# A graph-attention layer on one core: norm, softmax and attention of the next group moved to other stages, roots computed on VectorE

## The chip, the core and the metric

The kernel runs on one core of a Trainium2 chip. The metric is the device time of that core in microseconds (us), as a median of several executions; lower is better. The core has five engines that work side by side: TensorE (PE in the profile) multiplies matrices, VectorE (DVE) and ScalarE (ACT) do element-wise work, GpSimd (POOL) does element-wise work more slowly (a 128x512 sum takes 1.26 us there and 0.69 on VectorE), and SyncE (SP) issues transfers. TensorE writes into PSUM, which is cut into eight banks here: six large ones called "mm" and two small ones called "aux".

## The reference, cut to what matters

```
h = relu(layernorm(x))                       # x: 128 graphs x 64 nodes x 512, float32
h = elu(gat_heads(h, adj, W_heads, a_heads)) # 4 heads, each 512 -> 512
h = elu(gat_heads(h, adj, W_out, a_out))     # 2048 -> 512
y = relu(h @ w1 + b1) @ w2 + b2 + h
out = x + layernorm(y) * gamma + beta
# gat_heads: softmax over neighbours of leaky(f1_i + f2_j), times (h @ W)
```

## The kernel before

The 8192 rows are 64 tiles of 128, worked in 16 groups of four tiles. A group passes through a head stage (four heads, products called g_a) and a second projection (g_b), beside which the feed-forward products of the group before (g_c, g_d) run. Each large product is cut into seven Strassen-Winograd products (seven block products in place of eight); the seven accumulate in three PSUM banks, and the sum between products 6 and 7 is made in the bank:

```
order: 1, 5, 6, 2, 3, 7, 4     # the products of one head
own = {1: 1, 2: 1, 5: 5, 3: 5, 6: 6, 7: 6, 4: 6}   # which bank each accumulates in
def after(p):
    if p in (1, 5, 6):
        if p == 6:
            nc.vector.tensor_tensor(gb[6], gb[6], sb["s1"], ALU.add)   # VectorE
        nc.scalar.copy(sb[nm], gb[p])                                  # ScalarE
```

Product 7 accumulates in the bank of product 6. So TensorE, at the sixth product of a head, waits for the VectorE sum and the ScalarE copy behind the third. The profile prints the sum as `g_a<-g_a,s_a` and the copy as `t_a<-g_a`.

The norms, one tile at a time, with the root as a power on GpSimd:

```
def norm_stats(src, tag, t):
    nc.vector.bn_stats(st, src); nc.vector.bn_aggr(mv, st)
    nc.vector.tensor_scalar(ve, mv[:, 1:2], EPS, None, ALU.add)
    nc.gpsimd.tensor_tensor(rstd, ve, mhalf, ALU.pow)
```

The first attention of a tile pair, in two banks at a time of the six:

```
banks = [bank(f"pz{nm}_{t}_{b}") for b in range(NB)]        # "mm", six banks
... 64-row matmuls of the two graphs of the tile ...
nc.scalar.copy(...) for b == 0; nc.vector.tensor_copy(...) for b == 1
```

Of the kernel before, what the change touches and what calls it, by code (L numbers as in the profile page):

```python
# [9 lines left out]
FP = mybir.dt.float32  # L10
# [8 lines left out]
AHEAD = 150  # L19


@with_exitstack
def gat_preln_kernel(
# [47 lines left out]
    ring = ctx.enter_context(tc.tile_pool(name="ring", bufs=11))  # L71
# [20 lines left out]
    def load(t, name="x"):  # L92

        tl = wk.tile([P, F], FP, tag="x", name=f"{name}{t}", bufs=4)
        nc.sync.dma_start(out=tl, in_=xf[ts(t, P), :])
        return tl
# [47 lines left out]
    MT, TC = {}, {}  # L144
    DIRECT = {}

    def fetch(m):
        MT[m] = big.tile([P, KC, O], FP, tag=homes[m], name=f"pw{m}")
        queue = nc.scalar if m < H else nc.gpsimd
        queue.dma_start(out=MT[m], in_=mats[m].rearrange("(k p) o -> p k o", p=P))  # L150
# [13 lines left out]
    def turn_a():  # L164

        rows = H * 2 * KC
        pt = aux([P, rows], "pah")
        nc.tensor.transpose(pt, ah, ident[0:rows, 0:rows])
        aT = wk.tile([P, H, 2, KC], FP, tag="s1", name="aT")
        nc.scalar.copy(aT.rearrange("p h c o -> p (h c o)"), pt)  # L170
        return aT

    def fold_dve(m, ab):

        for k in range(KC):
            for c in range(2):
                junk = wk.tile([P, O], FP, tag="t", name=f"jk{c}_{m}_{k}")
                nc.vector.scalar_tensor_tensor(
                    junk, MT[m][:, k, :], 1.0, ab[c], ALU.mult, ALU.mult,
                    accum_out=wa[:, k, c * H + m:c * H + m + 1],  # L180
                )
# [17 lines left out]
    def weight_sums(m, after=None):  # L199
# [20 lines left out]
        TC[m] = [dram.tile([P, 2, 2, Q], FP, name=f"tc{m}_{i}") for i in range(2)]  # L220
# [19 lines left out]


    late = []
# [17 lines left out]
    def unit(name, product, post, order):  # L260
# [5 lines left out]
        def after(p):  # L266
            if p in (1, 5, 6):
                nm = {1: "s1", 5: "s5", 6: "t"}[p]
                sb[nm] = wk.tile([P, 2, T], FP, tag=nm, name=f"{nm}_{name}")
                if p == 6:  # L270

                    nc.vector.tensor_tensor(gb[6], gb[6], sb["s1"], ALU.add)
                nc.scalar.copy(sb[nm], gb[p])
                post(nm, sb[nm])
            elif p == 2:
                post("c11", gb[1])
            elif p == 7:
                post("c22", gb[6], sb["s5"], gb[1])
            elif p == 3:
                post("c12", gb[5], sb["t"], gb[5])  # L280
            else:
                post("c21", gb[6])
# [17 lines left out]
    def product_t(m, blocks):  # L300

        def product(p):
            def fn(bk, start):
                w, a = piece(m, p), blocks(p)
                for o in range(2):
                    for k in range(2):
                        nc.tensor.matmul(  # L307
# [6 lines left out]
    def product_n(ms, blocks):  # L314

        def product(p):
            def part(i):
                def fn(bk, start):
                    w, a = piece(ms[i], p), blocks(p, i)
                    for k in range(2):  # L320
                        for j in range(2):
                            nc.tensor.matmul(  # L322
# [17 lines left out]
    def norm_stats(src, tag, t):  # L340

        st = sm.tile([P, 6], FP, tag=tag + "st", name=f"{tag}st{t}")
        nc.vector.bn_stats(st, src)
        mv = sm.tile([P, 2], FP, tag=tag + "mv", name=f"{tag}mv{t}")
        nc.vector.bn_aggr(mv, st)
        ve = sm.tile([P, 1], FP, tag=tag + "ve", name=f"{tag}ve{t}")
        nc.vector.tensor_scalar(ve, mv[:, 1:2], EPS, None, ALU.add)  # L347
        rstd = sm.tile([P, 1], FP, tag=tag + "rs", name=f"{tag}rs{t}")
        nc.gpsimd.tensor_tensor(rstd, ve, mhalf, ALU.pow)
        return mv[:, 0:1], rstd  # L350

    def norm1(t):
        if t not in X:
            X[t] = load(t)
        mean, rstd = norm_stats(X[t], "n1", t)
        nb = sm.tile([P, 1], FP, tag="n1nb", name=f"n1nb{t}")
        nc.gpsimd.tensor_scalar(nb, mean, rstd, -1.0, ALU.mult, ALU.mult)
        HN[t] = big.tile([P, F], FP, tag="hn", name=f"hn{t}", bufs=G)
        nc.scalar.activation(HN[t], X.pop(t), AF.Relu, bias=nb, scale=rstd)
        if t % G >= 2:  # L360
            HNS[t] = big.tile([P, T], FP, tag="hns", name=f"hns{t}", bufs=2)
            nc.gpsimd.tensor_tensor(HNS[t], HN[t][:, 0:T], HN[t][:, T:2 * T], ALU.add)
# [12 lines left out]
    def project_f(g):  # L375
# [15 lines left out]
        eng = nc.vector if g == 0 else nc.gpsimd  # L391
        eng.tensor_tensor(
# [65 lines left out]
    A1, E1, LAST = {}, {}, {}  # L458
# [4 lines left out]
    def transpose_weights(p):  # L463
        A = A1.pop(p)
        for j in range(2):
# [7 lines left out]
            AT[t] = big.tile([P, NB, H, N], FP, tag="at", name=f"at{t}", bufs=G)  # L473
# [6 lines left out]
    def stage_a(g):  # L480


        if g >= NG:
            return [], [], []
        p, r = 2 * g, 2 * g + 1

        def norms(p):
            norm1(2 * p)
            norm1(2 * p + 1)
            if p >= 2:  # L490
                prefetch(2 * p + 2)
                prefetch(2 * p + 3)

        def transposes(p):
            transpose_h(2 * p)
            transpose_h(2 * p + 1)

        return (
            [lambda: norms(p), lambda: norms(r)],
            [  # L500
                lambda: transposes(p), lambda: transposes(r), nothing, lambda: project_f(g), nothing,
                lambda: (scores1(g), attn_weights(p)), nothing, lambda: attn_weights(r),
            ],
            [nothing, lambda: transpose_weights(p), nothing, nothing, lambda: transpose_weights(r)],
        )
# [4 lines left out]
    def attend1(g):  # L510
# [3 lines left out]
        def task(j, half):  # L514
# [6 lines left out]
            banks = [bank(f"pz{nm}_{t}_{b}") for b in range(NB)]  # L521
# [8 lines left out]
            for b in range(NB):  # L530
# [3 lines left out]
                if b == 0:  # L534
# [28 lines left out]
    def project1(g, h):  # L563
# [11 lines left out]
        def post(what, a, b=None, to=None):  # L575
# [8 lines left out]
            if what == "c21":  # L584
                nc.gpsimd.tensor_tensor(dst, dst, H1["22"][:, h], ALU.add)  # L585

# [15 lines left out]
    WH2 = {}  # L602

    def project2(g):
        slot = {1: "11", 2: "12", 3: "12", 4: "22", 5: "S1", 6: "11", 7: "S1"}
        h1 = dict(H1)
        wh = big.tile([P, G, FO], FP, tag="wh2", name=f"wh2_{g}")
        WH2[g] = wh

        def post(what, a, b=None, to=None):  # L610
            behind = {"s1": ("11", "S1", "11"), "s5": ("S1", "22", "11"), "c11": ("12", "12", "11")}
            if what in behind:
                dst, x0, x1 = (h1[n] for n in behind[what])
                for h in range(H):
                    nc.gpsimd.tensor_tensor(dst[:, h], x0[:, h], x1[:, h], ALU.subtract)  # L615
# [11 lines left out]
            f"b{g}", product_n(ms, lambda p, i: h1[slot[p]][:, i]), post, (1, 5, 6, 2, 7, 3, 4)  # L627
# [5 lines left out]
    def scores2(g, j):  # L633
# [3 lines left out]
        for c in range(2):  # L637
            junk = wk.tile([P, FO], FP, tag="elu", name=f"jf{g}_{j}_{c}", bufs=3)
            nc.vector.scalar_tensor_tensor(  # L639
                junk, WH2[g][:, j], 1.0, ao[:, c, :], ALU.mult, ALU.mult,  # L640
# [30 lines left out]
    def attend2(g, j):  # L671
        pa = aux([P, FO], f"pa2_{g}_{j}")
        nc.tensor.matmul(pa, AT2[g][:, j, :], WH2[g][:, j, :], start=True, stop=True)  # L673
# [16 lines left out]
    def feed_forward(g):  # L690
# [42 lines left out]
        def post2(what, a, b=None, to=None):  # L733
# [5 lines left out]
            eng = nc.vector if what[0] == "c" else nc.gpsimd  # L739
            eng.tensor_tensor(dst, a, dst, ALU.add)  # L740

        def finish(j):
            t = G * g + j
            xr = load(t, "xr")
            nc.gpsimd.tensor_tensor(xr, xr, bs, ALU.add)
            y = o[:, j]
            mean, rstd = norm_stats(y, "n2", t)
            nc.vector.scalar_tensor_tensor(y, y, mean, gs, ALU.subtract, ALU.mult)
            nc.vector.scalar_tensor_tensor(y, y, rstd, xr, ALU.mult, ALU.add)
            nc.sync.dma_start(out=of[ts(t, P), :], in_=y)  # L750

        f1 = unit(f"c{g}", product_t(M1, lambda p: bl[1][p]), post1, (1, 5, 6, 2, 3, 7, 4))
        f2 = unit(f"d{g}", product_n([M2], lambda p, i: bl[2][p]), post2, (1, 5, 6, 2, 3, 7, 4))
        return (
            [lambda j=j: transpose_out(j) for j in range(G)], f1 + f2,
            [lambda j=j: finish(j) for j in range(G)],
        )

    def mix(*lists):

        lists = [l for l in lists if l]
        keyed = [((i + 0.5) / len(l), n, fn) for n, l in enumerate(lists) for i, fn in enumerate(l)]
        return [fn for _, _, fn in sorted(keyed, key=lambda k: k[:2])]
# [4 lines left out]
    for t in range(G):  # L768
        norm1(t)
# [47 lines left out]
    for g in range(NG):  # L817
        if g >= 1:
            side = stage_e(g - 1)
        else:  # L820
            side = sum(stage_a(1), [])
            for i, m in ((5, 4), (9, 5), (12, 6), (17, 7)):
# [11 lines left out]
        attn = attend1(g + 1) if g + 1 < NG else []  # L834
        norms, scores, turns = stage_a(g + 2)
        tr, ff, fin = feed_forward(g - 1) if g >= 1 else ([], [], [])
        if g == NG - 1:
            run(project2(g), tr + [nothing] * 6 + ff[:2])
# [6 lines left out]
        early = [lambda: z_sums(g + 1, 0)]  # L845
        first = mix(attn, tr)
        if g >= 1:
            first[5:5] = norms[:1]
            first[10:10] = norms[1:]
        if g == 0:  # L850
            def sums_late(m):
# [3 lines left out]
            run(project2(g), first + early + norms + scores + turns + [  # L855
                load_rows, lambda: sums_late(M1), lambda: sums_late(M2)
            ])
        else:
            run(project2(g), first + mix(
                ff[:7] + early + ff[7:12] + fin[:1] + ff[12:13] + fin[1:2] + ff[13:],  # L860
                scores + [nothing] * 8,
            ) + mix(fin[2:], [nothing] + turns + [nothing] * 2))
    last = fin
    tr, ff, fin = feed_forward(NG - 1)
    run(tr + ff[:6] + last + ff[6:12] + fin[:2] + ff[12:] + fin[2:])
# [29 lines left out]
```

## Time and profile before

| | |
|---|---|
| time | 2363.31 us (2363.18 to 2363.83, 3 runs) |
| TensorE busy | 2317.9 of 2360.4 us |
| one group in the middle | 142.96 us |

The prediction below shows the main lines. Three more stretches stand behind the prediction: start-up to the first g_a product, group 0, and a later group. Columns are start:end, length, then busy time and count of PE, PEld (weight loads), DVE, ACT and POOL, granted clock, DMA share, GB/s. The granted clock is to be read with care: a stretch for which the trace holds no clock record reads 1.00 (more on this below).

```profile
0.00:54.58 54.58, 35.24 (x166) 23.88 (x166) 38.77 (x107) 15.07 (x27) 33.48 (x49) 0.75 0.88 319
54.58:190.57 135.99, 126.89 (x713) 104.41 (x714) 65.45 (x113) 52.41 (x93) 84.31 (x85) 0.97 0.49 164
2049.05:2186.07 137.02, 137.02 (x655) 115.14 (x654) 61.95 (x107) 47.72 (x85) 53.32 (x42) 1.00 0.45 149
```

Group 14 has 655 matmul records where a middle group has 736, and takes 5.9 us less. The kernel before works on scores two groups ahead, so here, near the end, nothing is left to prepare.

### The profile page before, as it was taken

Reading aid. Unit: us, or ns where it says so; the run is one execution under the profiler, and the core shown is the slowest. Engines: PE = TensorE matmul, PEld = TensorE weight load, DVE = VectorE, ACT = ScalarE, POOL = GpSimd, SP = SyncE. Lnnn points to the kernel's source line nnn. Section 1 sums busy time; section 2 is a strip of 40 time slices with the busy share of each in tenths; the row PEclk is TensorE's granted clock in tenths of the full one; section 3 lists DMA queues with packets and bytes.
Section 4 is the critical chain, followed back from the end, with each engine's and each line's share of the span. In section 5 each row is a group of like instructions: output and inputs, shape, how many; then the busy total and the mean of one; then the engine's idle time right before and its main releaser. Section 6 shows DMA issues by size and latency. Waiting matters only on the chain.

```text
span 2360.4 us, 32849 instructions
## 1 busy us (share of the span) xinstructions
PE 2317.9 (98%) x11805; PEld 1934.5 (82%) x11805; DVE 1265.5 (54%) x2210; ACT 911.0 (39%) x1623; POOL 1026.7 (43%) x917
## 2 busy tenths in 40 slices
PE   6989999999999999999999999999999999999997
PEld 4868787888878888787887878888788887878885
DVE  7625474554646556474554745556464563744527
ACT  2524425253352533425244251533525344251513
POOL 5664444416344353443524444253443534533333
PEclk7999999999999999999999999999999999999999
DMA  8545353444535445353444544435354453534443
GB/s 308 184 142 193 125 183 127 164 152 132 182 125 178 134 139 179 126 180 129 154 163 129 182 131 161 153 130 181 127 177 132 138 179 127 182 118 164 157 148 106
DMA packets 257809, 366.89 MB, mean 155 GB/s; under 512 B 22216, under 2 KB 145128, under 8 KB 257648
## 3 DMA queue, kind: packets, MB, share of 16 engines
q1 hardware_dynamic: 251024, 343.82, 43.9%
q0 software_dynamic: 4512, 16.78, 1.9%
q10 hardware_dynamic: 2112, 4.19, 0.5%
q8 instruction: 95, 1.56, 0.3%
q14 instruction: 66, 0.54, 0.1%
HBM read 337.45 MB, written 27.26 MB: 155 GB/s over the span
## 4 chain that ended last, share of the span: by engine, by line
PE 94%; DVE 2%; ACT 1%; POOL 1%; issue 0%; DMA 0%; DVEq 0%
PE g_b L322 33%; PE g_a L307 32%; PE g_c L307 8%; PE g_d L322 8%; PE pz L525 4%; PE pa L673 2%; PE pto L700 1%; PE pzS L525 1%; PE pth L371 1%; PE s1pt L472 1%; PE pf L381 1%; PE s1pe L406 1%; DMA x<-in_x_dram 0%; PE s2pt L667 0%; PE pwa L193 0%
## 5 line engine op out<-in xcount | busy, mean ns | idle before, releaser
L322 PE MATMUL g_b<-w,h 128*128 128x256 f32 x2560 | 598.1, 381 | 0.0
L322 PEld LDWEIGHTS g_b<-w,h 128*128 128x128 f32 x2560 | 480.5, 190 | 72.2 <-issue 10.1
L307 PE MATMUL g_a<-z,w 128*128 128x256 f32 x1520 | 361.0, 380 | 1.2 <-DVE g_a L581 0.7
L307 PE MATMUL g_a<-zs_z,w 128*128 128x256 f32 x1504 | 347.9, 379 | 0.0
L307 PEld LDWEIGHTS g_a<-z,w 128*128 128x128 f32 x1520 | 287.6, 190 | 57.9 <-issue 14.3
L307 PEld LDWEIGHTS g_a<-zs_z,w 128*128 128x128 f32 x1504 | 284.8, 190 | 50.5 <-issue 14.3
L322 PE MATMUL g_b<-w,hS 128*128 128x256 f32 x1024 | 243.5, 382 | 0.0
L585 POOL TENSOR_TENSOR hS<-hS,h 128x512 f32<-128x512 f32 x64 | 83.0, 1297 | 366.8 <-DVE hS L549 366.8
L547 ACT ACTIVATE exc<-g_a 128x512 f32<-128x512 f32 x256 | 152.3, 595 | 199.7 <-DVE g_a L581 119.6
L322 PEld LDWEIGHTS g_b<-w,hS 128*128 128x128 f32 x1024 | 191.4, 191 | 30.9 <-issue 6.7
L549 DVE SCALAR_TENSOR_TENSOR h<-exc,g_a 128x512 f32<-128x512 f32 x192 | 131.6, 686 | 136.3 <-ACT exc L548 136.2
L548 ACT ACTIVATE exc<-exc 128x512 f32<-128x512 f32 x256 | 161.6, 631 | 6.5
L615 POOL TENSOR_TENSOR h<-h,h 128x512 f32<-128x512 f32 x64 | 86.7, 1362 | 138.1 <-PE g_b L322 138.0
L332 POOL TENSOR_TENSOR zs_z<-zS,z 128x512 f32<-128x512 f32 x63 | 89.7, 1424 | 128.3 <-PE g_a L307 123.7
L615 POOL TENSOR_TENSOR h<-hS,h 128x512 f32<-128x512 f32 x64 | 81.1, 1268 | 142.4 <-PE g_b L322 142.4
L474 ACT COPY at<-s1pt 128x512 f32<-128x512 f32 x64 | 34.7, 588 | 279.8 <-PE s1pt L472 279.8
L307 PE MATMUL g_c<-ot,w 128*128 128x256 f32 x512 | 123.9, 385 | 0.8 <-DVE n2ve L347 0.8
L322 PE MATMUL g_d<-w,rt 128*128 128x256 f32 x512 | 121.5, 380 | 1.7 <-DVE o L740 1.0
L307 PE MATMUL g_a<-zS,w 128*128 128x256 f32 x496 | 117.2, 379 | 0.0
L639 DVE SCALAR_TENSOR_TENSOR jf<-wh,ao 128x512 f32<-128x512 f32 x128 | 94.3, 776 | 40.3 <-ACT wh L621 40.1
L333 POOL TENSOR_TENSOR zs_z<-z,zs_z 128x512 f32<-128x512 f32 x63 | 85.4, 1357 | 61.1 <-PE g_a L307 40.7
L307 PEld LDWEIGHTS g_c<-ot,w 128*128 128x128 f32 x512 | 93.9, 190 | 21.8 <-issue 9.3
(159 smaller groups left out, 3535.6 us busy)
## 6 DMA issues: line engine op xcount, KB each, us to landing
w<-tc SPq DMA_DIRECT2D x632, 256.0 KB, 2.6
w<-in_L_gnn_W_heads_dram SPq DMA_DIRECT2D x192, 256.0 KB, 2.7
w<-in_L_gnn_W_out_dram SPq DMA_DIRECT2D x192, 256.0 KB, 2.7
w<-in_L_gnn_w_dram SPq DMA_DIRECT2D x96, 256.0 KB, 2.7
x<-in_x_dram SPq DMA_DIRECT2D x66, 256.0 KB, 3.6
xr<-in_x_dram SPq DMA_DIRECT2D x64, 256.0 KB, 2.8
out_dram<-o SPq DMA_DIRECT2D x64, 256.0 KB, 2.1
tc<-pt POOLq DMA_DIRECT2D x20, 512.0 KB, 5.6
```

Of the source, the lines that this page charges most:

```text
L307: nc.tensor.matmul(bk[:, o, :], w[:, k, ts(o, P)], a[:, k, :], start=start and o == 0 and k == 0, stop=k == 1, skip_group_check=True,)
L322: nc.tensor.matmul(bk[:, j, :], a[:, k, ts(j, P)], w[:, k, :], start=start and k == 0 and j == 0, stop=i == len(ms) - 1 and k == 1, skip_g ...
L332: eng.tensor_tensor(s2, s1, a11, ALU.subtract)
L333: eng.tensor_tensor(s4, a12, s2, ALU.subtract)
L525: nc.tensor.matmul(banks[b][:, c, :].rearrange("p (h n) -> p h n", h=H), src[rows, off + c * P:off + (c + 1) * P], at[rows, b], start=True ...
L547: nc.scalar.activation(ex, src, AF.Relu, scale=-1.0)
L548: nc.scalar.activation(ex, ex, AF.Exp, scale=-1.0)
L549: nc.vector.scalar_tensor_tensor(dst, ex, -1.0, src, ALU.add, ALU.max)
L585: nc.gpsimd.tensor_tensor(dst, dst, H1["22"][:, h], ALU.add)
L615: nc.gpsimd.tensor_tensor(dst[:, h], x0[:, h], x1[:, h], ALU.subtract)
L639: nc.vector.scalar_tensor_tensor(junk, WH2[g][:, j], 1.0, ao[:, c, :], ALU.mult, ALU.mult, accum_out=f[:, c, j:j + 1],)
L673: nc.tensor.matmul(pa, AT2[g][:, j, :], WH2[g][:, j, :], start=True, stop=True)
```

## The change

The intent: give the softmax and the attention of the next group more room, prepare one group ahead instead of two, and take the roots off GpSimd. The core of the diff, cut:

```diff
-        rstd = sm.tile([P, 1], FP, tag=tag + "rs", name=f"{tag}rs{t}")
-        nc.gpsimd.tensor_tensor(rstd, ve, mhalf, ALU.pow)
+        nc.vector.tensor_scalar(v, mv[:, :, 1], EPS, None, ALU.add)
+        nc.vector.tensor_scalar(hv, v, -0.5, None, ALU.mult)
+        yi, vi = y.bitcast(mybir.dt.int32), v.bitcast(mybir.dt.int32)
+        nc.vector.tensor_scalar(yi, vi, 1, None, ALU.logical_shift_right)
+        nc.vector.tensor_scalar(yi, yi, -1.0, float(0x5F3759DF), ALU.mult, ALU.add)
+        for _ in range(3):
+            nc.vector.tensor_tensor(u, y, y, ALU.mult)
+            nc.vector.tensor_tensor(u, u, hv, ALU.mult)
+            nc.vector.scalar_tensor_tensor(y, u, 1.5, y, ALU.add, ALU.mult)
 ... (norms of four tiles at once, in place; output norms two tiles at once)
-            banks = [bank(f"pz{nm}_{t}_{b}") for b in range(NB)]
+            banks = [aux([P, 2, T], f"pz{nm}_{t}_{b}") for b in range(NB)]
-                if b == 0:
+                if b == 0 or g > 0:
                     nc.scalar.copy(dst, srcv)
 ... (product R and the last sums of the feed-forward: GpSimd -> VectorE)
+            if g + 1 < NG:
+                side.insert(15, lambda: norms1(g + 1, True))      # norm in the head stage
 ...
+        tasks = attention_tasks(g + 1)        # transposes, scores, softmax: first half
+        for i, fn in enumerate(attn):
+            tasks.append((0.55 + 0.05 * i, fn))                   # attention: second half
+            tasks += [(0.84, fin[0]), (0.97, fin[1])]             # output norms, in pairs
```

Tiles of x are now loaded into the buffers of the norm and no longer share the ones ("x") of the residual rows. A deeper form of the second projection is in the file but switched off.

## The prediction

> **What bounds the kernel now.** I read the page first, then the busy time by stretch, then the list of who waited for whom on TensorE, and last the timeline of single stages. The page:
>
> ```profile
> span 2360.4 us, 32849 instructions
> PE 2317.9 (98%) x11805; PEld 1934.5 (82%) x11805; DVE 1265.5 (54%) x2210; ACT 911.0 (39%) x1623; POOL 1026.7 (43%) x917
> PE   6989999999999999999999999999999999999997
> ...
> PE 94%; DVE 2%; ACT 1%; POOL 1%; issue 0%; DMA 0%; DVEq 0%
> ```
>
> TensorE is busy 98% of the span and carries 94% of the chain; only the first slices and the last are not full. The stretches (start:end, length, then busy time of each engine) say where the missing time is:
>
> ```profile
> 0.00:64.50 64.50, 43.98 (x221) 30.98 (x222) 44.62 (x120) 21.57 (x38) 35.73 (x54) 0.79 0.80 289
> 64.50:190.70 126.20, 118.29 (x657) 97.44 (x658) 59.61 (x101) 45.91 (x82) 82.06 (x81) 0.97 0.50 168
> ...
> 333.70:476.65 142.95, 142.95 (x735) 119.72 (x735) 78.01 (x134) 56.73 (x101) 60.51 (x53) 1.00 0.45 151
> 476.65:619.60 142.95, 142.95 (x736) 119.71 (x735) 78.13 (x134) 56.72 (x101) 60.48 (x53) 1.00 0.46 152
> ...
> 2318.00:2360.40 42.40, 28.73 (x131) 22.44 (x129) 30.49 (x52) 9.57 (x19) 19.93 (x17) 0.94 0.28 100
> ```
>
> From the second group on each group of four tiles takes 142.95 us and TensorE is busy for all of it. The waits of TensorE for the stretch 333.7 to 2100 us come back empty. What it waits for in the whole run is in the first 160 us and the last 42:
>
> ```profile
> PE pzS L525 <- DVE z L537: 5.5, 1, 5.5
> PE s1pt L472 <- DVE s1A L435: 5.4, 1, 5.4
> PE pab L158 <- DMA ar<-in_L_gnn_a_heads_dram: 5.4, 1, 5.4
> ...
> PE pth L371 <- ACT hT L373: 1.7, 1, 1.7
> ```
>
> So a faster vector engine or GpSimd can gain nothing in the middle 2,100 us. The change can gain only TensorE work, or the 20.5 us idle in the start-up, the 7.9 us in group 0 and the 13.7 us in the tail, and it can lose by making a wait where there is none.
>
> **What the Trainium skill says.** "TensorEngine Tiling (Array Packing)", Key Properties: changing the tiling mode drains TensorE. The trace agrees: a unit of 8 full-array matmul records takes 1.73 us (476.49 to 478.21), but 1.92 us in front of an attention task with 64-row tiles (533.87 to 535.79). "SBUF — State Buffer", Who interferes with whom: a VectorE instruction with two SBUF inputs contends with a GpSimd instruction that reads SBUF, and so do two-port modes. The trace agrees, even for tiny operands:
>
> ```profile
> 12.86 1.11 DVE L122 TENSOR_TENSOR headrow<-id 128x4 f32<-128x4 f32 x1
> ...
> 16.36 1.33 DVE L135 TENSOR_TENSOR eye<-ident 128x64 f32<-128x64 f32 x1
> ```
>
> Each ends when the GpSimd sum beside it (1.26 us) ends. "Perfetto Trace Analysis", Optimizing Scalar/DVE Operations: every VectorE instruction has a fixed overhead. Here 128x1 ones last 0.15 us and a dependent next one starts 0.21 to 0.24 us later (statistics at 4.51 us, next at 4.73), while a 128x512 one takes 0.69.
>
> **The change, part by part.** The deep form of the second projection is switched off (its threshold 99 is above all 16 groups), so its code counts for nothing.
>
> *TensorE work.* The built programs hold the same 6,327 matmuls of the same shapes, and 122 runs of 64-row attention matmuls in both, so the drains are the same. The work per group stays at 142.95 us: change 0.
>
> *Roots.* 128 powers on GpSimd (0.55 us, 0.99 under contention) and 64 products go. They become chains of 13 small VectorE instructions (add, scale, shift, multiply-add, three Newton rounds of three), with one more for the norm: at 0.21 us some 2.9 us a chain, one chain per group for the input norm and two for the output norm, so 8.5 us per group, less 1.2 us for the old adds. Half of the attention copies go from VectorE to ScalarE (8 x 0.68 = 5.4 us per group), the broadcast product R (1.04 on GpSimd) and two output sums come to VectorE. VectorE goes from 78 to about 83 us of 143: not a bound in sum. Instructions rise by some 700 on VectorE.
>
> *Norm in the head stage.* Statistics, one chain and four activations (0.81 us each) now stand in the third head, between the ELU work. They are gated behind the last, late product of the second head. The sensitive place is the two small PSUM banks in which the second attention (pa) lands:
>
> ```profile
> 510.17 1.02 PE L673 MATMUL pa<-wh,at 128*128 128x512 f32 x2
> 514.10 0.68 DVE L549 SCALAR_TENSOR_TENSOR o<-ex,pa 128x512 f32<-128x512 f32 x1
> 518.79 1.02 PE L673 MATMUL pa<-wh,at 128*128 128x512 f32 x2
> ```
>
> The bank of the first pa is free at 514.8 and wanted again at 518.8: 4.0 us of slack. In the new order ScalarE puts three norm activations, two ELU passes, a fourth activation and a copy between the two passes of that ELU. By hand from the row durations: gate 505.2, statistics and the ELU sums to 511.7, nine chain links of 0.21 to 513.5, three activations (start to start 0.71) to 515.7, ELU, activation, ELU, copy to 517.9, second pass 518.5, VectorE 519.2. So TensorE would wait 0.4 us, and with restart some 0.7 us. Links of 0.15 make it 0, links of 0.30 make it about 1.5.
>
> *First half of the second projection.* Transposes of the output (pto) and of the next norm (pth) now alternate in the same two banks, 0.43 us of other matmuls apart, while a ScalarE copy takes 0.58 plus 0.25 to start. By the same hand working two waits of 0.1 to 0.3 us: 0.3 us per group. The softmax has 19 us from scores to transposes and needs some 7: no wait.
>
> *Second half.* Attention tasks use the same two banks, both copied by ScalarE (1.2 us plus 0.3), with 1.73 us of matmuls at the closest place and 3.5 to 5.2 elsewhere: no wait.
>
> Steady sum: about 0.9 us in each of 14 groups, 12 us (estimate, 0 to 28).
>
> *Start-up.* Four tiles' roots in one chain need all four loads (11.8 us) and run against the GpSimd weight sums; some 20 VectorE instructions that contend, one per sum, may move the 24 weight products from 17.8 to 20-23 us. The first projection of scores has 2.6 us of slack (products end 33.1, wanted 35.7): 0 to 3 us. Then the first attention has two banks instead of six, and the next group's tiles load into buffers that are only free after it, with their statistics ahead of the copies in VectorE's order: some 5 us. Together about +6.5.
>
> *Group 0.* The long wait was a queue:
>
> ```profile
> 104.38 24.35 SPq L238 DMA_DIRECT2D w<-tc  x8
> ...
> 129.31 0.41 SPq L95 DMA_DIRECT2D x<-in_x_dram  x1
> ```
>
> The input tile stood behind eight weight blocks that GpSimd finishes late; its statistics held the copies that attention needed. In the new kernel no input tile of the next norm is wanted there, so 5.5 + 1.7 us and a few small ones go; but the weight blocks may be late themselves. -8.
>
> *Tail.* After the last matmul two chains of 13 and eight large operations stand on VectorE alone, about 11.5 us where 8.9 are now: +2.5.
>
> Sum: 12 + 6.5 - 8 + 2.5 = 13 on the median 2363.3, so 2376; since every loss is hand work on thin margins and the compiled order was made by a scheduler that saw no such waits, I take 3 off: 2373.
>
> **Rivals.** (a) No new waits in the steady groups: for it, all margins but one are positive by a microsecond; then start-up, group 0 and tail cancel and the time is 2358 to 2366. (b) ScalarE or VectorE holds the pa bank for longer: for it, that order is the same in all 14 groups and contention adds 1.1 us to a link; against it, GpSimd is nearly idle in the head stage (11.7 us of 52). At 2 to 3 us per group: 2395 to 2410. (c) The output norm's chain delays the first head's sums at the end of the second projection, as GpSimd is busy there: the chain has 5 us of margin; beyond it 1 us per group is 14 us. (d) A real gain beyond 2%: only 42 us of TensorE idle exist in all, and 47 would be needed; impossible without less TensorE work.
>
> **Range and chances.** 2357 (no steady waits, group 0 all gained) to 2395 (2 us per group). Beyond the upper end 2% (2410.6) needs 3 us per group. Faster 0.01, within 0.94, slower 0.05.
>
> **What would show it.** TensorE's busy time near 2318 again, and its waits in the middle of the run: pa waiting for VectorE's o, 14 times, and pto or pth waiting for ScalarE. Period 143 to 145 us. No wait of pzS for VectorE near 136 us; the first full matmul later than 54.6 us; GpSimd's busy time down by about 150 us. I am wrong if the period is 142.95 exactly (rival a), or over 145 (b or c), or if the start-up is not longer.

## The result, and the profile after

| | before | after |
|---|---|---|
| median | 2363.31 us | 2402.06 us (2399.31 to 2403.88, 3 runs) |
| ratio | | 1.0162 (1.0139 to 1.0185) |
| span of the profiled run | 2360.4 us | 2401.8 us |

Ratios here and below are the mean time of one kernel's fast runs over that of the other's of the same rounds, so not quite the ratio of the medians. The kernel became 1.6% slower: above the predicted range (2357 to 2395).

The page after:

```profile
span 2401.8 us, 33093 instructions
PE 2340.1 (97%) x11805; PEld 1936.3 (81%) x11805; DVE 1338.6 (56%) x2649; ACT 965.6 (40%) x1743; POOL 880.5 (37%) x678
PE   5999999999999999999999999999999999999997
```

The number of matmuls is the same, yet TensorE is "busy" 22 us longer. Part of a wait or of a slow clock can hide in a busy time whose ends are modelled, so I went by the times at which each stage starts. The same stretches as before:

```profile
0.00:70.94 70.94, 43.49 (x165) 29.13 (x166) 46.10 (x107) 14.40 (x25) 32.69 (x39) 1.00 0.70 245
70.94:202.65 131.71, 126.92 (x633) 103.12 (x633) 54.40 (x85) 48.56 (x86) 83.45 (x73) 0.99 0.57 186
...
490.21:634.47 144.26, 143.47 (x736) 119.16 (x735) 82.65 (x162) 60.20 (x109) 51.47 (x39) 1.00 0.48 150
...
2077.17:2221.45 144.28, 143.46 (x736) 119.16 (x735) 82.00 (x162) 60.33 (x109) 51.39 (x39) 1.00 0.45 142
2221.45:2401.80 180.35, 161.39 (x733) 135.85 (x731) 99.08 (x219) 58.09 (x106) 50.71 (x39) 0.97 0.42 131
```

Set against the kernel before, the 41.4 us between the spans fall into five parts:

| stretch | before | after | difference |
|---|---|---|---|
| start-up, to the first g_a | 54.58 | 70.94 | +16.4 |
| group 0 | 135.99 | 131.71 | -4.3 |
| groups 1 to 13 | 1858.48 | 1874.52 | +16.0 |
| group 14 | 137.02 | 144.28 | +7.3 |
| group 15 and tail | 174.33 | 180.35 | +6.0 |

Groups 0 and 14 belong together. The matmuls that the earlier kernel does in group 0 for group 2 are done later now, 5.9 us of them, and group 14 is no longer short.

What TensorE waits for, from the list of its waits (engine, line, what was waited for: us in all, times, longest):

```profile
PE g_a L365 <- issue: 11.3, 14, 0.8
PE s1pe L488 <- DVE R L474: 6.0, 1, 6.0
...
PE pth L454 <- ACT hn L440: 3.6, 1, 3.6
```

The first line repeats in each of 14 groups, always 9.6 us after the head stage begins. "issue" means that the profile found no releaser. The timeline around one of them (start, duration, engine, line, instruction) shows it:

```profile
487.90 2.94 POOL L925 TENSOR_TENSOR xr<-xr,bs 128x512 f32<-128x512 f32 x2
489.63 1.23 DVE L421 TENSOR_SCALAR n2v<-n2mv 128x2 f32<-128x2 f32 x1
490.78 1.83 DVE L929 SCALAR_TENSOR_TENSOR o<-o,n2mv,gs 128x512 f32<-128x512 f32 x1
490.80 2.94 POOL L392 TENSOR_TENSOR zs_z<-z,zs_z 128x512 f32<-128x512 f32 x2
492.53 1.23 DVE L422 TENSOR_SCALAR n2h<-n2v 128x2 f32<-128x2 f32 x1
...
495.63 0.16 DVE L429 SCALAR_TENSOR_TENSOR n2y<-n2u,n2y 128x2 f32<-128x2 f32 x1
495.83 1.42 DVE L930 SCALAR_TENSOR_TENSOR o<-o,n2y,xr 128x512 f32<-128x512 f32 x2
...
498.39 0.69 DVE L330 TENSOR_TENSOR g_a<-g_a,s_a 128x512 f32<-128x512 f32 x1
499.12 0.58 ACT L331 COPY t_a<-g_a 128x512 f32<-128x512 f32 x1 [4.61 <-DVE g_a L330]
499.80 1.53 PE L365 MATMUL g_a<-zs_z,w 128*128 128x256 f32 x6 [0.80 <-issue]
```

Product 6 of the first head is done at about 495.6, and product 7, which needs its bank, was due at 498.84 (the fifth product starts at 497.12 and takes 1.73). VectorE works its instructions off one after the other, as the timeline shows, and has first the chain of the output norm, two output rows and two score products. It comes to the sum at 498.39; ScalarE copies until 499.70; TensorE starts at 499.80, about 1 us late. The chain itself took from 489.63 to 495.8, 6.2 us, where 13 links of 0.21 would be 2.7. Three VectorE instructions explain the rest: n2v and n2h on 128x2 elements last 1.23 us instead of 0.16, and `o` 1.83 instead of about 0.75. n2v and n2h end within 0.02 us of the end of a GpSimd sum (490.84 and 493.74). `o` gets in between the two sums of a pair: the first ends at 492.06, `o` at 492.61, and the second, held meanwhile, lasts 1.72 us instead of 1.26.

In the kernel before, the same sum ran at 481.94, 5.45 us into the stage; now it comes 8.2 us into it. Since TensorE is about 1 us late, the sum would have had to begin by about 7.2: from 5.45 there was room for some 1.8 us, and the chain with what stands behind it took 2.7.

The start-up has the same pattern, and one more:

```profile
15.17 4.31 DVE L429 SCALAR_TENSOR_TENSOR n1y<-n1u,n1y 128x4 f32<-128x4 f32 x1
...
15.75 1.27 POOL L235 TENSOR_TENSOR pt<-pw,pt 128x512 f32<-128x512 f32 x1
16.97 1.27 POOL L236 TENSOR_TENSOR pt<-pw 128x512 f32<-128x512 f32 x1
18.20 1.26 POOL L237 TENSOR_TENSOR pt<-pw,pt 128x512 f32<-128x512 f32 x1
...
44.23 4.91 POOL L925 TENSOR_TENSOR xr<-xr,bs 128x512 f32<-128x512 f32 x4
45.22 4.48 DVE L474 TENSOR_TENSOR R<-U,headrow 128x512 f32<-128x512 f32 x1
...
59.08 11.93 PE L594 MATMUL pz<-at,hn 64*128 64x256 f32 x32
```

One link on four elements lasts 4.31 us: it gets through when a row of three GpSimd sums ends. The product R lasts 4.48 us (0.66 in the kernel before) beside four residual sums. Those belong to the output norm of group 0, 200 us later; since x and residual rows no longer share buffers, nothing holds them back, and the scheduler put them here. Lastly the first 32 attention matmuls take 11.9 us; before, with six banks, they took 5.3:

```profile
49.05 5.28 PE L525 MATMUL pz<-at,hn 64*128 64x256 f32 x32
```

The single records of the trace show why. Before, the two row halves start together (two at 49.05, two at 49.63), first every 0.43 us and from 51.3 us on every 0.21 us. After, the halves for the most part come one after the other, each when its bank has been copied, and records keep 0.43 us throughout; the full g_a products behind them run at that slow rate too, until 75.8.

So the 16.4 us of the start-up split by start times: the first score projection (pf) 41.81 instead of 35.69, +6.1; from there to the score matmuls 8.04 instead of 4.12, +3.9; from the first pz to the first g_a 11.86 instead of 5.53, +6.3.

About half of the first term does not belong to the change as such. The start-up up to pf is the same code in the changed kernel and in xr_late below; in the profiled run of xr_late pf came at 38.87. The same matmuls in front of it, first in the changed kernel, then in xr_late:

```profile
29.72 2.07 PE L176 MATMUL pab<-ar,ident 8*128 8x512 f32 x2
32.63 3.41 PE L211 MATMUL pwa<-aT,wT 128*128 128x2 f32 x16
```

```profile
29.55 1.12 PE L176 MATMUL pab<-ar,ident 8*128 8x512 f32 x2
31.09 2.02 PE L211 MATMUL pwa<-aT,wT 128*128 128x2 f32 x16
```

The trace of xr_late records a granted clock of 1.00 from 29.21 to 32.62 us and 0.50 after it; that of the changed kernel has no clock record before 75.8. In the profiled runs of pow_out, xr_late, newton6 and r_gpsimd such a short stretch begins at 28.8 to 30.0 us and pf comes at 38.7 to 38.9; in those of the changed kernel, six_banks and fin_later there is none and pf comes at 41.7 to 41.9. So 3.0 of the 6.1 us come and go between executions of the same code. The other 3.1 go with the first weight product on VectorE, which begins at 20.92 instead of 17.76.

### The profile page after: what moved, and what is told of

It is laid out like the page before. It is cut to its first block, busy times and chain, and to the rows that moved or that the text cites. A ratio compares the mean times of both kernels' runs of the same rounds, so it can differ in the third digit from the quotient of the medians.

```text
span 2401.8 us, 33093 instructions
## 1 busy us (share of the span) xinstructions
PE 2340.1 (97%) x11805; PEld 1936.3 (81%) x11805; DVE 1338.6 (56%) x2649; ACT 965.6 (40%) x1743; POOL 880.5 (37%) x678
## 4 chain that ended last, share of the span: by engine, by line
PE 95%; DVE 3%; issue 1%; DMA 0%; ACT 0%; POOL 0%; SPq 0%; DVEq 0%; ACTq 0%; POOLq 0%
PE g_b L380 33%; PE g_a L365 32%; PE g_d L380 8%; PE g_c L365 8%; PE pz L594 5%; PE pa L851 2%; PE pzS L594 1%; PE s1pt L554 1%; PE pth L454 1%; PE pto L880 1%; PE s1pe L488 1%; PE pf L464 1%; DMA hn<-in_x_dram 0%; PE s2pt L845 0%; PE pwa L211 0%
## 5 line engine op out<-in xcount | busy, mean ns | idle before, releaser
L380 PE MATMUL g_b<-w,h 128*128 128x256 f32 x2560 | 612.1, 382 | 0.0
L380 PEld LDWEIGHTS g_b<-w,h 128*128 128x128 f32 x2560 | 470.8, 190 | 81.2 <-issue 24.5
L365 PEld LDWEIGHTS g_a<-z,w 128*128 128x128 f32 x1520 | 289.5, 191 | 57.9 <-issue 11.4
L380 PE MATMUL g_b<-w,hS 128*128 128x256 f32 x1024 | 238.0, 381 | 0.0
L604 ACT COPY z<-pz 128x512 f32<-128x512 f32 x186 | 100.1, 588 | 210.5 <-PE pz L594 210.5
L925 POOL TENSOR_TENSOR xr<-xr,bs 128x512 f32<-128x512 f32 x64 | 88.1, 1389 | 135.6 <-DMA xr<-in_x_dram 108.5
L816 DVE SCALAR_TENSOR_TENSOR jf<-wh,ao 128x512 f32<-128x512 f32 x128 | 128.5, 1049 | 14.0 <-ACT wh L798 13.3
L882 POOL TENSOR_TENSOR o<-o,b2s 128x512 f32<-128x512 f32 x64 | 88.1, 1378 | 124.0 <-PE pto L880 70.6
L686 POOL TENSOR_TENSOR hS<-h,h 128x512 f32<-128x512 f32 x64 | 86.0, 1348 | 115.8 <-PE g_b L380 115.8
L594 PE MATMUL pz<-at,hn 64*128 64x256 f32 x768 | 118.2, 413 | 0.0
```

The costliest lines, as they stand in the source:

```text
L365: LAST["pe"] = nc.tensor.matmul(bk[:, o, :], w[:, k, ts(o, P)], a[:, k, :], start=start and o == 0 and k == 0, stop=k == 1, skip_group_che ...
L380: LAST["pe"] = nc.tensor.matmul(bk[:, j, :], a[:, k, ts(j, P)], w[:, k, :], start=start and k == 0 and j == 0, stop=i == len(ms) - 1 and k ...
L594: nc.tensor.matmul(banks[b][:, c, :].rearrange("p (h n) -> p h n", h=H), src[rows, off + c * P:off + (c + 1) * P], at[rows, b], start=True ...
L604: nc.scalar.copy(dst, srcv)
L686: nc.gpsimd.tensor_tensor(dst[:, h], x0[:, h], x1[:, h], ALU.subtract)
L816: nc.vector.scalar_tensor_tensor(junk.rearrange("p (c v o) -> p c v o", c=2, v=2), WH2[g][j], 1.0, ao[:, c, :].rearrange("p (c v o) -> p c ...
```

## The experiments

Theory A: chains of small VectorE instructions are held out by GpSimd's sums and stand in front of sums that free banks. Theory B: the new order of norm, softmax and attention costs it, whatever computes the roots. Twelve kernels ran; all gave correct results, and each is compared with the kernel before on the same chip (2363.7 to 2364.6 us). The edits are cut to their core.

| run | us | ratio to before | range of runs |
|---|---|---|---|
| pow_both | 2387.27 | 1.0097 | 2380.20 to 2389.51 |
| pow_out | 2382.15 | 1.0095 | 2379.36 to 2398.04 |
| six_banks | 2389.86 | 1.0122 | 2389.00 to 2403.88 |
| xr_late | 2401.06 | 1.0156 | 2396.96 to 2403.39 |
| newton6 | 2521.49 | 1.0674 | 2519.04 to 2530.80 |
| newton_in_before | 2405.37 | 1.0170 | 2399.65 to 2407.89 |
| fin_later | 2440.68 | 1.0329 | 2436.23 to 2449.28 |
| r_gpsimd | 2409.28 | 1.0195 | 2406.46 to 2413.63 |
| mended | 2377.56 | 1.0055 | 2368.58 to 2381.43 |
| mended2 | 2380.83 | 1.0074 | 2380.54 to 2382.29 |
| mended3 | 2374.85 | 1.0041 | 2368.38 to 2375.16 |
| stats_late | 2353.06 | 0.9955 | 2352.02 to 2354.31 |

### The roots as powers again: both, and the output norm's alone

```diff
         nc.vector.tensor_scalar(v, mv[:, :, 1], EPS, None, ALU.add)
+        if tag in ("n1", "n2"):                  # pow_out: ("n2",)
+            for i in range(n):
+                nc.gpsimd.tensor_tensor(y[:, i:i + 1], v[:, i:i + 1], mhalf, ALU.pow)
+            return mv[:, :, 0], y
```

> The changed kernel with both roots as powers on GpSimd again, all else as changed. Theory A (the chains of small VectorE instructions stall behind GpSimd's sums and stand in front of the sums that free banks): the wait of 0.96 us in each head stage goes, so the period falls from 144.27 to 143.2-143.4 us; the norm activations of the start-up begin near 15 us instead of 21.0 and the first full g_a matmul comes at 64-67 us instead of 70.9; time 2370 to 2382. Theory B (the new order of norm, softmax and attention costs it, whatever computes the roots): period stays at 144.3, time 2395 to 2402.

> Only the output norm's root as a power on GpSimd, the input norm's stays on VectorE. Theory A, with the output norm's chain as the one that delays the first head's sum: period 143.2-143.4, last stretch 2 to 4 us shorter, start-up unchanged (first full g_a matmul at 70.9); time 2383 to 2389. If it is the input norm's chain or the order: period 144.3 and 2398 to 2403.

The stretch of one middle group, first of pow_both, then of pow_out, with its last stretch:

```profile
483.26:626.45 143.19, 143.19 (x736) 119.31 (x735) 71.53 (x125) 60.06 (x109) 54.23 (x47) 1.00 0.46 151
```

```profile
485.45:628.67 143.22, 143.22 (x736) 119.23 (x734) 73.30 (x137) 60.46 (x109) 51.92 (x43) 1.00 0.47 151
2206.38:2381.50 175.12, 159.89 (x733) 134.60 (x731) 88.80 (x157) 58.27 (x106) 57.12 (x49) 0.98 0.41 136
```

For the middle groups theory A holds in numbers: the output norm's chain alone makes the steady wait. Giving it back takes 1.05 us from an undisturbed group, 11.4 us from groups 1 to 14 together (three of them still wait, up to 0.5 us) and 5.2 us from the last stretch (180.35 to 175.12). The spans of the two profiled runs differ by 20.3 us; 3.1 of them lie in the start-up and are the clock of the paragraph above, not the root. The period stays 0.25 us above the old 142.96.

For the start-up theory A was wrong. With both powers the norm activations began at 15.4 us as expected (21.0 changed, 14.0 before), yet the first g_a came at 70.35. What follows the activations had other holds: the first weight product on VectorE began at 20.3 us (17.8 before), since the mask instructions in front of it are small VectorE instructions too and wait for the same GpSimd sums. So in the start-up the input norm's chain cost little: with the same clock, pf came 0.6 us earlier without it (41.21 against 41.81). In the head stage of group 0, where the input norm of group 1 stands, it did cost: that part of group 0 took 61.18 us in pow_both and 65.73 in pow_out, and the waits of TensorE for n1nb (1.1 us) and for the weight sums of GpSimd (1.9) are gone. The runs of pow_both scatter over 9 us and those of pow_out over 19, and the median of pow_both lies above that of pow_out although it has one part more given back; in the profiled runs it is 3.1 us below. The next run shows a reason for such scatter.

### Six banks for the first attention

```diff
-            banks = [aux([P, 2, T], f"pz{nm}_{t}_{b}") for b in range(NB)]
+            banks = [(bank(f"pz{nm}_{t}_{b}") if g == 0 else aux(...)) for b in range(NB)]
```

> The changed kernel, but the first attention of group 0 alone takes the six large PSUM banks as before. If two banks are the reason that the 32 first pz matmuls take 11.9 us instead of 5.3: they take about 5.5 again, the first full g_a matmul comes at 64-65 us, and with the second half of that attention 6 to 10 us go: 2392 to 2396. If the copies on ScalarE and VectorE bound it: within 2 us of 2402.

The first g_a came at 64.68, 5.5 us behind the first pz, and four of five runs lie at 2389 to 2390.4: two banks cost 12 us, of which the trace shows 6.3 in the start-up and 4.8 in the head stage of group 0. The profiled run was the one at 2403.9, and shows where its gain went:

```profile
138.39 9.20 DVE L474 TENSOR_TENSOR R<-U,headrow 128x512 f32<-128x512 f32 x1
...
142.12 3.69 POOL L686 TENSOR_TENSOR h<-hS,h 128x512 f32<-128x512 f32 x3
145.78 2.92 POOL L686 TENSOR_TENSOR hS<-h,h 128x512 f32<-128x512 f32 x2
147.73 1.99 PE L488 MATMUL s1pe<-R,L 64*64 64x256 f32 x16 [7.05 <-DVE R L474]
```

R of group 1 began beside a row of eight GpSimd sums and got in between the seventh and the eighth, 9.2 us later; TensorE waited 7.05, and that half of group 0 took 75.29 us instead of 65.39. In the profiled run of the changed kernel the same R took 1.38 us. So whether R gets in is a matter of the moment. That the other long runs, such as the two of pow_out above 2395, are long for the same reason is not shown, as one run of each kernel was profiled.

### Residual sums held back

```diff
-            for x_ in xr:
-                nc.gpsimd.tensor_tensor(x_, x_, bs, ALU.add)
+            for i, x_ in enumerate(xr):
+                add = nc.gpsimd.tensor_tensor(x_, x_, bs, ALU.add)
+                if g == 0:
+                    behind_pe(add)          # waits for TensorE's place in group 1
```

> The changed kernel, but the four GpSimd sums of residual and beta of group 0 are held until group 1, where they are wanted. If they hold VectorE's product R (4.48 us, 0.66 before): R takes 0.7 us and 3 to 4 us go: 2398 to 2399. If R was slow by itself: no change.

R took 0.69 us and the score matmuls followed pf by 4.2 us, as before, so the cause of the 3.9 us is shown. The median did not move (2401.06): held until group 1, the sums came so late there that the head stage of group 2 waited 4.8 us at the same bank and took 58.0 us instead of 52.4. A gain of 3.9 us in the start-up was given back 280 us later by the mend itself, which cost 5.6.

### A longer chain

```diff
-        for _ in range(3):
+        for _ in range(6 if tag == "n2" else 3):
```

> The changed kernel with six Newton rounds in the output norm's chain instead of three: nine more links of about 0.2 us, so 1.8 us more in front of the first head's sum; nothing else changes. Theory A (this chain delays the sum that frees TensorE's bank, and its slack is used up): the wait in each head stage grows from 0.96 to about 2.7 us and the period from 144.27 to about 146, time 2422 to 2432. Theory that the wait comes from the new order or from an instruction fetch: period 144.3, time 2399 to 2405.

The direction was right and the size was far off: 2521 us. The waits of TensorE and two of the links:

```profile
PE g_a L365 <- issue: 93.4, 14, 6.8
```

```profile
501.88 1.27 POOL L925 TENSOR_TENSOR xr<-xr,bs 128x512 f32<-128x512 f32 x1
502.05 1.13 DVE L425 TENSOR_SCALAR n2y<-n2y 128x2 int32<-128x2 int32 x1
503.11 1.27 POOL L390 TENSOR_TENSOR zs_z<-zS,z 128x512 f32<-128x512 f32 x1
503.21 1.18 DVE L427 TENSOR_TENSOR n2u<-n2y 128x2 f32<-128x2 f32 x1
```

Nine links of 0.2 us made the wait grow by 5.9 us, not 1.8. The next residual sums now fall into the chain (in the changed kernel they stood before and behind it) and hold two more links, which makes 2.0 us, and the chain's second link starts 4.5 us into the stage instead of 2.3. I read this as a loop that keeps itself late, since a late output frees the residual buffers later; the loop is argued from the timeline, not tested. And behind a wait of 6.7 us TensorE's records run at 0.43 us instead of 0.22 for about ten records, some 2 us more; the granted clock of this trace reads 0.50 in just this stretch (510.12 to 516.94) and in one like it, of 7 or 10 us, in each group from 350 us on.

### The chain alone, in the kernel before

```diff
+        if tag == "n2":                       # per tile, in place of the power on GpSimd
+            ... the same 13 instructions on VectorE ...
+            return mv[:, 0:1], rstd
```

> The kernel before with one part of the change alone: the output norm's root as the Newton chain on VectorE, one chain per tile. If chains on VectorE alone make a wait whatever the order: the period rises from 142.95 by 0.5 to 3 us and the time is 2371 to 2405. If it takes the new order too: period 142.95 and only the last stretch grows, 2364 to 2368.

2405.37 us: this one part, in the old order, costs 42 us, as much as the whole change (in the profiled run 27.5 us in groups 1 to 13 and 14.6 in group 15 and the tail). TensorE waits at the very same place, and here the profile names the releaser:

```profile
PE g_a L307 <- ACT t_a L273: 23.3, 13, 4.0
```

But what holds the sum here is not what holds it in the changed kernel. One of the stages:

```profile
337.91 0.16 DVE L359 SCALAR_TENSOR_TENSOR n2rs<-n2u,n2rs 128x1 f32<-128x1 f32 x1
339.88 0.42 SPq L95 DMA_DIRECT2D x<-in_x_dram  x1
343.93 0.69 DVE L343 BATCH_NORM_STATS2 n1st<-x 128x6 f32<-128x512 f32 x1 [2.76 <-DMA x<-in_x_dram]
344.54 0.68 DVE L272 TENSOR_TENSOR g_a<-g_a,s_a 128x512 f32<-128x512 f32 x1
```

The chain's last link is done 2.5 us into the stage, at the usual 0.20 us from link to link. VectorE then stands idle for 2.76 us (2.1 to 4.8 in groups 2 to 13) at a statistic of the next norm, whose tile is late, and the sum stands behind it; without the idle time the sum, which came 8.5 to 11.4 us into the stage, would have come at 6.3 to 6.6 (an estimate), before the 7.2 at which it starts to cost. In the old order the tiles of x share their four buffers with the residual rows, and the two loads were issued only behind the late output rows that read those (336.90 and 339.88; in the kernel before from 331.65 on). So this run shows that the chain costs much in the old order too, but by a late load. That the change's order alone makes no steady wait is shown by pow_out, not by this run.

### The chains moved behind the first head's sum

```diff
-            tasks += [(0.84, fin[0]), (0.97, fin[1])]
+            carry = fin        # begun in the next head stage, behind its fifth and sixth product
```

> The changed kernel with the roots still on VectorE, but the output norms of a group are begun in the next group's head stage, behind the fifth and sixth product of its first head, so that their chains of small instructions stand after the first head's bank-freeing sum and not before it. If it is the place of the chain in VectorE's order that costs the wait: the wait of 0.96 us goes and the period is 143.2 to 143.6 us, time 2384 to 2392. If the mere work on VectorE costs it: 144.3 and 2399 to 2405. A new wait is possible where the next output needs the buffer: then above 2405.

(The edit also ties the statistics of the output norm to TensorE's place, in all but the last groups.) The old wait is gone and the kernel is slower still, 2440.68 us:

```profile
PE s2pt L845 <- DVE s2A L532: 27.2, 15, 2.5
PE g_a L365 <- DVE g_a L650: 9.6, 11, 1.1
```

The chains now delay the second softmax (s2A) and later sums of the head. Place alone is not the cure: I found no free place for a chain in the head stage, though VectorE is busy there only about half of the time.

### R on GpSimd

```diff
-        nc.vector.tensor_tensor(
+        (nc.vector if g == 0 else nc.gpsimd).tensor_tensor(
             R, U[...], headrow[...], ALU.mult)
```

> The changed kernel with R on GpSimd for all groups but the first, alone. If R on VectorE is held out by GpSimd's sums only now and then (1.4 us in the profiled run of the changed kernel, 9.2 in another): the median stays within 4 us of 2402 and the runs lie closer together. If it costs in most runs: 2392 to 2397.

It is slower, 2409.28. R takes 1.03 us there but waits its turn behind the sums, and TensorE waits 4.5 us for it in group 0 in the profiled run. Group 0 took 7.5 us more than in the changed kernel: the clock record reads 0.50 for 6.8 us behind the wait, which accounts for about the rest. My second guess (2392 to 2397) and my first (within 4 us) both missed. The runs did not lie closer together: they spread over 7 us, those of the changed kernel over 4.6.

### Mends together

> The changed kernel with three mends together: both roots as powers on GpSimd, the first attention of group 0 in six banks, the residual sums of group 0 held until group 1. If the parts add: first full g_a matmul near 60 us (70.35 with the powers alone, less 6.3 for the banks and 3.8 for R), period 143.2, time 2362 to 2372, so level with the kernel before. If something else in the start-up takes their place: 2375 or more.

> The changed kernel with five mends: both roots as powers on GpSimd, six banks for the first attention, the residual sums of group 0 held only until the first softmax is done, the products of the start-up in two junk buffers instead of one, and the product R on GpSimd for all groups but the first. The earlier set of three mends measured 2377.6 with R waits of 6.8 us in group 0 and a wait of 3.7 us in group 2 that came from holding the sums too long. If these two were the rest: first full g_a matmul at 55 to 58 us, no wait over 3 us after that but in the tail, 2358 to 2366. If not: 2370 or more.

> The changed kernel with both roots as powers on GpSimd, six banks for the first attention, the residual sums of group 0 held only until the first softmax is done, and two junk buffers in the start-up that share with nothing there (the earlier set shared one with the folded weights and waited 7.3 us for it); R stays on VectorE. If the earlier sets failed by what their own mends added: first full g_a matmul at 54 to 58 us, the wait of 3.7 us in group 2 gone, R's wait of up to 7 us in group 0 left to chance, 2360 to 2373. If the start-up keeps its 10 us otherwise: 2376 or more.

The first set (powers, six banks, residual sums held until group 1) gave 2377.56. Its first g_a came at 57.56, but R took 8.99 us in group 0, and for the held sums TensorE waited 3.7 us in group 2. The second set held the sums only until the first softmax, put R on GpSimd and used two junk buffers for the weight products, one of which shared a tag with the folded attention weights; TensorE waited 7.3 us for that, my own mistake, and 4.7 us for R: 2380.83. The third set, with junk buffers that share nothing and R on VectorE, gave 2374.85, and 2368.4 in the profiled run, where R took 1.22 us. Against the kernel before, that run's span has +6.6 us in the start-up, -12.7 in group 0, +5.3 in 13 groups, +6.2 in group 14 and +0.8 in the tail, so 6.2 in all. With most of the losses named and taken out, the new order comes within 0.4% of the old one (1.0041, 1.0027 to 1.0055). Whether the second junk buffer gained anything is not shown: pf came at 42.2 us with two and at 38.5 with one in the first set, but the trace of the first set has the short stretch at full clock (29.86 to 33.27 us) and that of the third has none, which alone makes 3 us.

### A kernel better than both

The prediction read a wait of 5.5 us in group 0 of the kernel before as a transfer queue. The profiled statistics belong to a tile of the third group ahead; they are not needed there at all. It is the pattern of the chain alone in the kernel before: a statistic that waits for its tile, with an urgent copy behind it. So they are held until group 1:

```diff
-        nc.vector.bn_stats(st, src)
+        stats = nc.vector.bn_stats(st, src)
+        if tag == "n1" and 3 * G <= t < 4 * G:
+            tc.add_manual_dep(stats.ins, LAST["pe"].ins.name, ...)
```

> The kernel before, but the statistics of the third group after next (tiles 12 to 15) are held until group 1, where they are wanted; before, one of them stands in front of the copies that attention needs at 136 us and waits for its tile. If that is the whole cause of the 5.5 us: no wait of pzS there, 5 to 8 us less, 2356 to 2359. If the copies would be late anyway: within 2 us of 2363.

2353.06 us, a ratio of 0.9955 (0.9943 to 0.9967): 10.7 us less, more than the expected 5 to 8, and the best of all kernels here. Group 0 shrank from 135.99 to 125.98:

```profile
54.11:180.09 125.98, 124.55 (x712) 102.90 (x713) 61.89 (x101) 52.48 (x93) 82.71 (x81) 1.00 0.53 177
```

The wait of pzS (5.5 us), that of the transposes behind it (1.7) and the slow records that followed the first (five or so at 0.21 extra) went. The middle groups did not change (142.96).

## Why the prediction was wrong, point by point

- **What bounds the kernel** was right: nothing to gain in the middle, and each new wait is a loss. **TensorE work per group, change 0**: nearly right; 0.25 us a group remain in pow_out. In the intervals of the trace the returns from 64-row attention to full products rose from four to eight per group, since output transposes no longer stand between, and a full product pays about 0.05 us more than a transpose there; this is argued from the intervals, not tested.
- **Norm in the head stage, the pa banks, 0.7 us**: this step failed. No wait of pa appears in the middle groups, nor the 0.3 us of pto and pth. The four activations fit. (VectorE's busy time per group came as worked out, 82.65 us for "about 83"; its instructions rose by 439, from 2210 to 2649, and not by "some 700".)
- **The steady sum, 12 us**: the size was near (16.0 in 13 groups), but for another reason, so the nearness is luck. This is the step that failed for the middle of the run. What happened is rival (c), the output norm's chain in front of the first head's sum. I had put it aside with "5 us of margin"; the traces leave some 1.8 us. I had counted the chain as 2.9 us and known the contention, but applied it to the start-up alone; three held instructions made it 6.2 us. The steps to blame are the link's price of 0.21 us, taken from a place where GpSimd was quiet, and the margin.
- **Start-up, +6.5**: measured +16.4. Two banks instead of six had the right mechanism and size (about 5 against 6.3). The term for contention, 0 to 3 us, measured 6.1 at pf in the profiled run, of which 3.0 are the clock that other executions of the same code had; the other 3.1 are the late first weight product, as said. pow_both shows that the input norm's chain is not what carried it (0.6 us). R, +3.9, was missing: residual sums that no buffer held back any longer.
- **Group 0, -8**: measured -4.3, and +7.3 in group 14. The waits at 136 us went as said ("a transfer queue" was right in that a late tile held VectorE; stats_late shows that the statistic could simply have come later). But I took the total of matmuls as proof that nothing moves, and did not see that 5.9 us of scores leave group 0 for group 14. For both groups together the step is +3.0 in place of -8. New waits in group 0 (1.9, 1.1 and 0.9 us in the list) took most of the rest; the first two go when the input norm's root is a power again, and group 0 is then 9.5 us shorter than before.
- **Tail, +2.5**: measured +6.0, of which 3.4 us after the last matmul (12.4 instead of 9.0). Two chains interleaved with large instructions there, and giving the output root back removed 5.2 us.
- **Three us off for thin margins**: it should have been the other way. All losses were found by hand on one order, and waits that I had not looked for were left.
- **Chances**: "within 2%" at 0.94 was the class that came; the range of 2357 to 2395 was too narrow by 7 us.

## What to carry to other kernels

Price a small VectorE instruction by what GpSimd does beside it, not by its own length: one of 0.16 us lasted 1.23 beside one sum and 4.3 us beside a row of three, a product of 0.66 us 9.2 beside a row of eight, and a chain of thirteen meets several. Before moving a root or any scalar chain onto an engine that also frees PSUM banks, find in its in-order queue the sum that TensorE waits for, and count what the chain puts in front of it. And when two kinds of tiles stop sharing buffers, look where the scheduler hoists the loads and sums that the sharing used to hold back. When they do share, a late output delays the next load, and whatever stands behind the instruction that waits for it. And before a difference in the start-up is given to a change, see whether the two executions had the same granted clock there.

## What the Trainium skill lacked or had wrong

- "SBUF — State Buffer", Who interferes with whom, says that whoever issues first holds the shared pair for the whole instruction and the other blocks. It does not say how long the other can be kept out beside a row of back-to-back GpSimd instructions. Here the waiting VectorE instruction was passed over at several gaps: a 128x4 instruction lasted 4.31 us beside three sums of 1.26 us, a 128x512 product 9.20 us (0.66 when GpSimd is quiet), getting in only at the seventh gap of a row of eight. In the middle groups `o` got in at the first gap, so this is no rule; what decides is not shown.
- The same section names two SBUF inputs and 2-port modes as what contends, and no size below which it stops. The trace agrees also for tiny operands: 128x2 scalar instructions, float32 (n2v, 1.23 us for 0.16) and int32 (1.13), and a product of a 128x2 tile with itself (1.18).
- "Perfetto Trace Analysis", Optimizing Scalar/DVE Operations, gives a fixed overhead for an instruction and advises to group. It lacks the price of a dependent chain: start to start 0.20 us for 128x2 links here, and contention on top.
- "TensorE: Matmul & The Clock Gate", What's actually happening, says that a cold array runs at half rate until about 3.4 us of sustained activity. The trace agrees with the factor (0.43 and 0.21 us per record). It does not say that alternating row halves may fail to count. In all seven profiled runs with two banks for the first attention the granted clock reached 1.00 only 14 to 17 us after the first of its matmuls, and 2.5 to 5.5 us after the full products that follow; in all seven with six banks, where both halves run together, after 1.7 to 3.8 us. Whether it is the half load or the short gaps between was not tested by itself.
- No page says how a profile shows a stretch without a clock record: it reads 1.00. The two-bank attention of the changed kernel and then that of pow_out, with records of 0.43 us in both:

```profile
59.00:70.90 11.90, 11.90 (x33) 8.61 (x32) 5.55 (x11) 3.55 (x6) 0.00 (x0) 1.00 0.09 22
```

```profile
56.00:67.80 11.80, 11.80 (x33) 8.63 (x32) 5.47 (x11) 3.56 (x6) 0.00 (x0) 0.50 0.09 22
```
